# Two edits to a four-layer network: one more product on VectorE in the last pair, and filter rows in four row groups

## The chip, the cores and the metric

The kernel runs on one core of a Trainium2 chip. The core has a matrix engine (TensorE, PE in the profile, with PEld for its weight loads), VectorE (DVE), ScalarE (ACT), GpSimd (POOL) and SyncE (SP), which here only issues transfers. Matmuls write PSUM, a memory taken here in banks of 128 partitions by 512 numbers. The metric is the time on the device in microseconds. Everything is in 32-bit floats.

## What is computed

Eight images of 64 channels and 64 x 64 pixels go through four layers: an attention layer over pixels, two blocks of windowed attention, a layer that filters each pixel with its own 3 x 3 filter (layer 2), and a state-space scan in four directions (layer 3). The change touches layers 2 and 3. Cut to what matters:

```python
# layer 2: nine filter weights for each pixel, times nine for each channel
s = jnp.einsum('bchw,tc->bthw', x, sw) + sb[None, :, None, None]
s = filter_norm(s, axis=1)             # minus the mean of the nine, over their deviation
...
cf = filter_norm(cf, axis=2)           # nine per channel, from the image's mean
for idx in range(TAPS):
    i, j = (idx // K, idx % K)
    out = out + xp[:, :, i:i + H, j:j + W] * s[:, idx:idx + 1] * cf[:, :, idx, None, None]

# layer 3: the scan along each of four directions k, with 16 states n per channel
def step(h, inp):
    u_t, dt_t, B_t, C_t = inp
    h = h * jnp.exp(dt_t[..., None] * A) + dt_t[..., None] * B_t[:, :, None, :] * u_t[..., None]
    return (h, jnp.einsum('bkcn,bkn->bkc', h, C_t))
```

## The kernel before

The images are taken in four pairs. For all of layers 0 to 2 a pair lies in 128 partitions, two images of 64 channels. Layer 3's scans take one image at a time, with its 128 inner channels.

**How the pairs are staggered.** The program first takes pair 0 through layers 0, 1 and 2 and the preparation of its scans, with part of pair 1's layer 0 beside it (`begin`, line 1168). Then, for each pair p, `scans` (line 1644) runs the scans of p, and between its steps it places the work of a second stream: `back` of pair p-1 (what follows the scans in layer 3) and `front` of pair p+1 (layers 0 to 2 and the scans' inputs). Beside the last pair's scans only `back` of pair 2 is left; `back` of the last pair runs alone at the end. The order in which instructions stand on each engine is then fixed by a scheduler when the program is built. It knows which instructions depend on each other and estimates their durations, so an edit can move instructions that it doesn't name.

**Layer 2** (`layer2` of the class `_Direct`, line 1526). It works in eight chunks of 512 pixels, eight rows of the image. In each chunk a matmul makes the centred filter weights, 9 for each of the two images and so 18 rows (`p_m`, line 1540). ScalarE squares them, a second matmul sums the squares (`p_v`, line 1544), four activations turn that into one over the deviation (lines 1547 to 1550), and VectorE makes the filter rows `f` (line 1552). Then there are nine taps. For each, a matmul with a matrix of zeros and constants, `pick`, spreads one row of `f` per image over that image's 64 channels (`pb`, line 1557). VectorE multiplies that with the shifted image and the channel's weight (`tap`, line 1560), and a matmul with the unit matrix adds it up in the bank `acc` (line 1561). After that a 1 x 9 convolution of nine matmuls follows (`py`, line 1571). The banks `p_m`, `p_v` and `pb` share three PSUM buffers, given out by `bank` (line 1199). The tables of the layer are loaded by `load` (line 240) on ScalarE's queue at the layer's start.

**The scans** (`scans` and `step`, line 1714). A unit is one direction k and one stretch of 512 pixels of one image; a unit has eight steps, each for two of the 16 states (j is 0 or 1), so that a pair has 64 units and 512 steps. For a step, SyncE fetches two rows of B and two of C from memory, each broadcast to all partitions (`fetch`, line 1702, 512 KB each; three buffers each), and POOL makes the product `vd` of B with dt times u for both states at once (`products`, line 1709, two steps ahead). For each state ScalarE makes the decay factors `dad` in a PSUM bank (line 1732), VectorE scans (line 1735), and ScalarE keeps the last value for the next unit (`carry`, line 1743). The result is multiplied with C, and TensorE adds it up over the 16 states in the bank `yd` with unit-matrix matmuls (`sums`, line 1762). At the end of a unit VectorE adds `yd` to the image's `Y`.

Who multiplies with C is what the change alters. In the first three pairs, in steps with even number, POOL takes both states in one instruction of 1024 columns (line 1746). In odd steps, and in all steps of the last pair, POOL takes state 0 (line 1748) and VectorE takes state 1 (line 1749). Where VectorE is to multiply, the scan writes over the decay factors in PSUM; where POOL is to, it writes the tile `hd` in SBUF, the memory beside PSUM. The banks of the decay factors come from three buffers, which also serve the two matmuls that prepare a unit (`pdd` and `pbc`).

The two statements in question:

```python
n0, rp = 2 * (i % 8), i % 2 or u["image"] >= B - 2
...
to = da if rp and j else h[:, j]
```

Of the kernel before, what the change touches and what calls it, by code (L numbers as in the profile page):

```python
# [17 lines left out]
P = 128  # L18
CH = 512
# [21 lines left out]
def _dup(a):  # L41
    a = np.asarray(a)
    return np.concatenate([a, a], axis=0)


def _blockdiag(a):
    a = np.asarray(a)
    r, c = a.shape
    out = np.zeros((2 * r, 2 * c), np.float32)
    out[:r, :c] = a  # L50
    out[r:, c:] = a
    return out
# [27 lines left out]

GENERAL = ("xpT", "dtT", "alog", "rpb0", "rpb1", "maskh", "maskv", "norm1_b0", "norm1_b1", "qb0", "qb1", "kb0", "kb1", "vb0", "vb1", "pb0", "pb1", "f1b0", "f1b1", "norm2_b0", "norm2_b1", "smask")
TEMP = ("swbd", "ds")
TABLES = ("cw2T", "pick")
TEMPW = ("xr", "drT", "alogs", "rpbT0", "rpbT1", "maskq", "b_all", "smask_t")


def _pack(w):
# [62 lines left out]
    e9 = np.eye(TAPS, dtype=np.float32)  # L152
    put("swbd", _blockdiag(f["sw"]))
    put("sb", _dup(_col(f["sb"])))
    put("cen9", _blockdiag(e9 - np.float32(1.0 / TAPS)))
    put("var9", _blockdiag(np.full((TAPS, TAPS), 1.0 / (TAPS - 1), np.float32)))
    put("cw1T", _dup(f["cw1"].T))
    mid = f["cw1"].shape[0]
    put("cb1", _col(f["cb1"]))
    put("cw2T", f["cw2"].reshape(C, TAPS, mid).transpose(2, 1, 0))  # L160
    pick = np.zeros((2 * TAPS, TAPS, P), np.float32)
    for im in range(2):
        for t in range(TAPS):
            pick[TAPS * im + t, t, 64 * im : 64 * im + 64] = np.sqrt(2.0) / 3
    put("pick", pick)
    put("cb2", _dup(f["cb2"].reshape(C, TAPS)))
    put("gmask", np.repeat(np.eye(2, dtype=np.float32) / L, 64, axis=0))
    w2 = f["w2"][:, :, 0, :]
# [41 lines left out]
    temp = [x for x in items[n_first:] if x[0] in TEMP]  # L210
    tempw = [x for x in items[n_first:] if x[0] in TEMPW]
    keep = [x for x in items[n_first:] if x[0] not in GENERAL + TEMP + TEMPW + TABLES]
    tables = [(n, sh, a[0 : 2 * TAPS]) for n, sh, a in items if n in TABLES]
    packs, layout = [], []
    for g, part in enumerate((items[:n_first], keep, temp, tempw, late, tables)):
        packs.append(np.ascontiguousarray(np.concatenate([x[2] for x in part], axis=1)))
# [10 lines left out]
class _Net:  # L227
# [45 lines left out]
    def prepare(self):  # L273
        nc, w, const = self.nc, self.w, self.const
        self.eps = const.tile([P, 5], F32, name="eps", tag="eps")
        for i, e in enumerate((LN_EPS, CN_EPS, BN_EPS, 1e-37, 1e-10)):
            nc.gpsimd.memset(self.eps[:, i : i + 1], e)
        eps_bn = self.eps[:, 2:3]

        bn1 = w["bn1"]  # L280
        sc = const.tile([P, 2, C], F32, name="bn1sc", tag="bn1sc")
        self.bn_fold((sc[:, 0, :], sc[:, 1, :]), bn1[:, 0, :], bn1[:, 1, :], bn1[:, 2, :], bn1[:, 3, :], eps_bn)
        self.w1a = const.tile([65, C], F32, name="w1a", tag="w1a")
        nc.vector.tensor_tensor(self.w1a[0:64, :], w["w1T"][0:64], sc[0:64, 0, :], ALU.mult)
        nc.vector.tensor_copy(self.w1a[64:65, :], sc[64:65, 1, :])

        self.w1bd = const.tile([P, P], F32, name="w1bd", tag="w1bd")
        nc.gpsimd.memset(self.w1bd, 0.0)
        for im in range(2):
            lo = slice(64 * im, 64 * im + 64)  # L290
            nc.vector.tensor_tensor(self.w1bd[lo, lo], w["w1T"][lo], sc[lo, 0, :], ALU.mult)
        self.b1row = const.tile([1, 2, C], F32, name="b1row", tag="b1row")
        nc.vector.tensor_copy(self.b1row, sc[0:1, 1, :].unsqueeze(1).to_broadcast([1, 2, C]))
        self.ones = const.tile([P, P], F32, name="ones", tag="ones")
        nc.gpsimd.memset(self.ones, 1.0)
        self.sums = const.tile([P, B // 2, 2, 32], F32, name="sums", tag="sums")

        bn = w["bn23"]
        self.bn23 = const.tile([P, 4], F32, name="bn23", tag="bn23")
        for i in range(2):  # L300
            self.bn_fold(
                (self.bn23[:, 2 * i : 2 * i + 1], self.bn23[:, 2 * i + 1 : 2 * i + 2]),
                *[bn[:, 4 * i + k : 4 * i + k + 1] for k in range(4)],
                eps_bn,
            )

        nr = 2 * TAPS

        self.swc = const.tile([P, nr], F32, name="swc", tag="swc")
        self.sbc = const.tile([nr, 1], F32, name="sbc", tag="sbc")  # L310
        with self.tc.tile_pool(name="psf", bufs=1, space=PSUM) as ps:
            pw = ps.tile([P, nr], F32, name="pswc", tag="pswc")
            nc.tensor.matmul(pw, lhsT=w["swbd"], rhs=w["cen9"], start=True, stop=True)
            nc.scalar.activation(self.swc, pw, AF.Copy)
            pb = ps.tile([nr, 1], F32, name="psbc", tag="psbc")
            nc.tensor.matmul(pb, lhsT=w["cen9"], rhs=w["sb"], start=True, stop=True)
            nc.scalar.activation(self.sbc, pb, AF.Copy)
        self.dsum = const.tile([P, 1], F32, name="dsum", tag="dsum")
        nc.vector.tensor_reduce(self.dsum, w["ds"], AX.X, ALU.add)
# [523 lines left out]
    def layer2(self, X):  # L843
# [5 lines left out]
        with ExitStack() as st:  # L849
# [7 lines left out]
            for c in range(NCH):  # L857
                cols = slice(c * CH, (c + 1) * CH)

                pm = ps.tile([nr, CH], F32, name="ps_m", tag="mm")  # L860
                nc.tensor.matmul(pm, lhsT=self.swc, rhs=X[:, cols], start=True, stop=True)
                q = wk.tile([nr, CH], F32, name="q2", tag="q2")
                nc.scalar.activation(q, pm, AF.Square, bias=self.sbc)
                pv = ps.tile([nr, CH], F32, name="ps_v", tag="pv")
                nc.tensor.matmul(pv, lhsT=w["var9"], rhs=q, start=True, stop=True)

# [3 lines left out]
                nc.scalar.activation(d, d, AF.Ln, bias=self.eps[0:nr, 4:5])  # L870
                nc.scalar.activation(d, d, AF.Exp, scale=-1.0)
                f = wk.tile([nr, CH], F32, name="f2", tag="f2")
                nc.vector.scalar_tensor_tensor(f, pm, self.sbc, d, ALU.add, ALU.mult)

                acc = ps.tile([P, 8, 64], F32, name="acc", tag="acc", bufs=1)
                for t in range(TAPS):
# [272 lines left out]
class _Direct:  # L1149
# [376 lines left out]
    def layer2(self, X):  # L1526
# [6 lines left out]
        with tc.tile_pool(name="w2", bufs=2) as wk:  # L1533
            net.load(wk, (5,))
            cf = net.channel_filters(X, wk, self.pf, "f")
            for c in range(NCH):
                x = X[:, c * CH : (c + 1) * CH]

                pm = self.bank("p_m", (nr, CH))
                nc.tensor.matmul(pm, lhsT=net.swc, rhs=x, start=True, stop=True)  # L1540
                q = wk.tile([nr, CH], F32, name="q2", tag="q2")
                nc.scalar.activation(q, pm, AF.Square, bias=net.sbc)
                pv = self.bank("p_v", (nr, CH))
                nc.tensor.matmul(pv, lhsT=w["var9"], rhs=q, start=True, stop=True)

                d = wk.tile([nr, CH], F32, name="d2", tag="d2")
                nc.scalar.activation(d, pv, AF.Ln, bias=net.eps[0:nr, 3:4])
                nc.scalar.activation(d, d, AF.Exp, scale=0.5)
                nc.scalar.activation(d, d, AF.Ln, bias=net.eps[0:nr, 4:5])
                nc.scalar.activation(d, d, AF.Exp, scale=-1.0)  # L1550
                f = wk.tile([nr, CH], F32, name="f2", tag="f2")
                nc.vector.scalar_tensor_tensor(f, pm, net.sbc, d, ALU.add, ALU.mult)

                acc = self.total("acc", (P, 8, 64))
                for t in range(TAPS):
                    pb = self.bank("pb", (P, 8, 64))
                    nc.tensor.matmul(pb, lhsT=w["pick"][:, t, :], rhs=f, start=True, stop=True)
                    src = XP[:, 8 * c + t // 3 : 8 * c + t // 3 + 8, t % 3 : t % 3 + 64]
                    tap = wk.tile([P, 8, 64], F32, name="tap", tag="tap", bufs=3)
                    nc.vector.scalar_tensor_tensor(tap, src, cf[:, t : t + 1], pb, ALU.mult, ALU.mult)  # L1560
                    nc.tensor.matmul(acc, lhsT=w["ident"], rhs=tap, start=(t == 0), stop=(t == TAPS - 1))
                    yield 2.3
# [151 lines left out]
    def step(self, i, st):  # L1714
# [3 lines left out]
        u = self.units[i // 8]  # L1718
        k, c, at, CC, v = u["k"], u["c"], u["at"], st["C"], st["v"]

        n0, rp = 2 * (i % 8), i % 2 or u["image"] >= B - 2
        rev = k >= 2

        def along(t):
# [4 lines left out]
        for j in range(2):  # L1729
            n = n0 + j  # L1730
            da = self.bank("dad", (P, TD), "da")
            nc.scalar.activation(da, u["du"][:, 0], AF.Exp, scale=net.As[:, k, n : n + 1])  # L1732
            first = 0.0 if at == 0 else self.carries[:, n : n + 1]
            to = da if rp and j else h[:, j]
            nc.vector.tensor_tensor_scan(along(to), along(da), along(v[:, j]), first, ALU.mult, ALU.add)  # L1735
            hs.append(to)
            if at < NTD - 1 and (rp or j):
                ends = h[:, :, 0] if rev else h[:, :, TD - 1]
                cs = self.carries[:, n0 : n0 + 2]
                if rp:  # L1740
                    ends = to[:, 0:1] if rev else to[:, TD - 1 : TD]
                    cs = self.carries[:, n : n + 1]
                nc.scalar.activation(cs, ends, AF.Copy)  # L1743

        if rp == 0:
            st["w"] = nc.gpsimd.tensor_tensor(v, h, CC, ALU.mult)  # L1746
        else:
            st["w"] = nc.gpsimd.tensor_tensor(v[:, 0], h[:, 0], CC[:, 0], ALU.mult)  # L1748
            nc.vector.tensor_tensor(v[:, 1], hs[1], CC[:, 1], ALU.mult)  # L1749

    def sums(self, i, st, after=None):

# [181 lines left out]
```

## Time and profile before

| | |
|---|---|
| median of 3 runs | 13789.17 us (13784.27 to 13789.92) |
| the profiled execution | 13842.86 us, its span 13841.1 us |
| TensorE busy | 11209.6 us, 81% of the span |
| VectorE busy | 8419.5 us, 61% |
| GpSimd busy | 8170.1 us, 59% |
| ScalarE busy | 7076.0 us, 51% |
| pair 0 without scans beside it | from 0 to about 2200 us |
| scans of pairs 0, 1, 2, 3 begin | about 2212, 4728, 8086, 11451 us |
| last pair's scans end, its `back` begins | 13587 us |

The page's 40 slices of 346 us each show how the load moves between engines:

```profile
PE   9999986888887679989888667997898767666665
DVE  0121336777668773366666766337665777987875
POOL 0000005888778755566666775547665688878982
PEclk9999977898898889998888788998888888888887
```

Each digit is the busy share of a slice in tenths, and PEclk is the clock granted to TensorE, in tenths of full speed. Slices 5 and 6 (counted from 1) hold pair 0's layer 2; the stretch from slice 34 on holds the last pair's scans, and the last slice mostly its `back`. A busy share is the union of an engine's instructions in the slice, so it says how long an engine had something running, not how fast that ran. The scans' four stretches can be told by the 512 products with B that POOL makes in each: 512 before 4727.5 us, 512 up to 8085.5, 512 up to 11450.5 and 512 after.

### The profile page before, as it was taken

What the parts mean: (1) busy time and instruction counts of PE and PEld (TensorE: products, weight loads), DVE (VectorE), ACT (ScalarE), POOL (GpSimd) and SP (SyncE); (2) the same over time, 40 slices, a digit from 0 to 9 for tenths busy, and PEclk for the clock granted to TensorE, in tenths of its full rate; (3) what the DMA queues carried; (4) which work ended last, traced back from release to release, by engine and by line L of the source; (5) the groups of instructions that cost most, each with busy time, mean ns of one, the idle gap of its engine ahead of it and who ended that gap; (6) DMA issues with size and microseconds to landing.
All of it is one profiled execution on the core that took longest, in us unless ns stands there. A gap on an engine that the chain in (4) does not pass through costs nothing. (4 is left out here: it accounts for less than half of the span.)

```text
span 13841.1 us, 141364 instructions
## 1 busy us (share of the span) xinstructions
PE 11209.6 (81%) x46358; PEld 4137.2 (30%) x46358; DVE 8419.5 (61%) x9763; ACT 7076.0 (51%) x15475; POOL 8170.1 (59%) x4111
## 2 busy tenths in 40 slices
PE   9999986888887679989888667997898767666665
PEld 2243322334232222224432222223443222222221
DVE  0121336777668773366666766337665777987875
ACT  5556514565536545555544545555554544454442
POOL 0000005888778755566666775547665688878982
PEclk9999977898898889998888788998888888888887
DMA  0000005666667754454554764335544577777882
GB/s 23 1 1 1 1 14 188 232 238 226 215 215 250 247 169 135 140 178 169 173 169 169 241 232 157 131 128 193 183 163 154 198 253 262 270 250 271 278 272 97
DMA packets 705785, 2383.41 MB, mean 172 GB/s; under 512 B 81092, under 2 KB 81220, under 8 KB 704012
## 3 DMA queue, kind: packets, MB, share of 16 engines
q1 hardware_dynamic: 681312, 2319.76, 49.3%
q10 hardware_dynamic: 23724, 54.50, 1.0%
q8 instruction: 367, 6.01, 0.2%
q14 instruction: 382, 3.13, 0.1%
HBM read 2271.18 MB, written 102.76 MB: 172 GB/s over the span
## 5 line engine op out<-in xcount | busy, mean ns | idle before, releaser
L1712 POOL TENSOR_TENSOR vd<-B,du 128x1024 f32<-128x1024 f32 x2048 | 4840.6, 2369 | 3889.7 <-DVE X L1352 2197.2
L1762 PE MATMUL yd<-vd,pack 128*128 128x512 f32 x8192 | 4637.8, 697 | 1386.2 <-POOL vd L1746 574.0
L1735 DVE TENSOR_TENSOR_SCAN hd<-dad,carry,vd 128x512 f32<-128x512 f32 x2464 | 3090.6, 1271 | 1024.6 <-ACT dad L1732 494.7
L1732 ACT ACTIVATE dad<-du,As 128x512 f32<-128x512 f32 x4096 | 2716.2, 680 | 1087.3 <-DVE hd L1735 761.8
L1762 PEld LDWEIGHTS yd<-vd,pack 128*128 128x128 f32 x8192 | 1633.4, 216 | 4072.9 <-issue 1829.8
L1746 POOL TENSOR_TENSOR vd<-hd,C 128x1024 f32<-128x1024 f32 x768 | 1811.9, 2359 | 1212.3 <-DVE hd L1735 618.7
L1748 POOL TENSOR_TENSOR vd<-hd,C 128x512 f32<-128x512 f32 x1280 | 1637.9, 1281 | 297.3 <-DVE hd L1735 217.9
L1302 ACT ACTIVATE e<-s 128x512 f32<-128x512 f32 x2048 | 1201.7, 592 | 1022.4 <-PE s L1296 1020.4
L1735 DVE TENSOR_TENSOR_SCAN dad<-dad,carry,vd 128x512 f32<-128x512 f32 x1120 | 1427.0, 1274 | 119.3 <-POOL vd L1712 79.4
L1296 PE MATMUL s<-X 64*128 64x512 f32 x4096 | 1325.4, 649 | 74.3 <-ACT e L1302 74.1
L1288 PE MATMUL po<-e,VT 128*64 128x512 f32 x4096 | 1197.7, 628 | 13.3 <-ACT e L1302 13.2
L1743 ACT ACTIVATE carry<-hd 128x1 f32<-128x1 f32 (+1 forms) x1792 | 357.7, 202 | 1222.9 <-DVE hd L1735 1218.5
L1749 DVE TENSOR_TENSOR vd<-dad,C 128x512 f32<-128x512 f32 x1280 | 859.7, 672 | 63.9 <-ACT carry L1743 54.0
L1296 PEld LDWEIGHTS s<-X 64*128 64x128 f32 x4096 | 360.1, 187 | 952.6 <-issue 786.1
L1450 PEld LDWEIGHTS w_av<-vals,w_e 64*64 64x64 f32 x16384 | 561.0, 147 | 196.4 <-issue 87.9
L1450 PE MATMUL w_av<-vals,w_e 64*64 64x9 f32 x16384 | 589.3, 208 | 25.5 <-ACT w_e L1440 25.4
L1435 DVE TENSOR_TENSOR w_e<-w_s,bias 128x512 f32<-128x512 f32 x512 | 329.5, 681 | 448.1 <-PE w_s L1423 447.6
L1735 DVE TENSOR_TENSOR_SCAN hd<-dad,vd 128x512 f32<-128x512 f32 x352 | 419.5, 1210 | 174.1 <-ACT dad L1732 78.1
L1440 ACT ACTIVATE w_e<-w_e 128x512 f32<-128x512 f32 x512 | 311.6, 627 | 377.5 <-DVE w_e L1435 265.8
L1743 ACT ACTIVATE carry<-dad 128x1 f32<-128x1 f32 x1120 | 189.1, 169 | 602.5 <-DVE dad L1735 600.3
L1687 PE MATMUL pdd<-xs,xdt 128*128 128x512 f32 x512 | 338.7, 749 | 185.1 <-DVE hd L1735 72.4
L1288 PEld LDWEIGHTS po<-e,VT 128*64 128x64 f32 x4096 | 221.6, 136 | 824.5 <-issue 774.2
(247 smaller groups left out, 10798.1 us busy)
## 6 DMA issues: line engine op xcount, KB each, us to landing
B<-rows SPq DMA_DIRECT2D x2048, 512.0 KB, 5.0
C<-rows SPq DMA_DIRECT2D x2048, 512.0 KB, 4.5
xs<-xt SPq DMA_DIRECT2D x128, 256.0 KB, 3.2
xs<-xc SPq DMA_DIRECT2D x128, 256.0 KB, 3.6
xc<-xcv ACTq DMA_DIRECT2D x64, 256.0 KB, 3.7
zs<-z ACTq DMA_DIRECT2D x64, 256.0 KB, 4.3
xt<-XT ACTq DMA_DIRECT2D x32, 512.0 KB, 7.1
rows<-bc SPq DMA_DIRECT2D x256, 64.0 KB, 2.0
```

The source lines that it names most:

```text
L1288: nc.tensor.matmul(po[half[im]], lhsT=VT[:, t, half[im]], rhs=es[im], start=(t == 0), stop=(t == 31))
L1296: nc.tensor.matmul(ss[im], lhsT=at(half[im], t), rhs=X[half[im], jc * CH : (jc + 1) * CH], start=True, stop=True)
L1302: nc.scalar.activation(e, ss[im], AF.Exp, scale=C**-0.5, accum_out=parts[:, im, t, jc : jc + 1])
L1450: nc.tensor.matmul(self.av[half[im], x % 4 + j, h, :], lhsT=es[h // 4][half[im], j, h % 4, :], rhs=V[half[im], x + j, h, :], start=True, s ...
L1712: self.nc.gpsimd.tensor_tensor(v, st["B"], dx.to_broadcast([P, 2, TD]), ALU.mult)
L1732: nc.scalar.activation(da, u["du"][:, 0], AF.Exp, scale=net.As[:, k, n : n + 1])
L1735: nc.vector.tensor_tensor_scan(along(to), along(da), along(v[:, j]), first, ALU.mult, ALU.add)
L1743: nc.scalar.activation(cs, ends, AF.Copy)
L1746: st["w"] = nc.gpsimd.tensor_tensor(v, h, CC, ALU.mult)
L1748: st["w"] = nc.gpsimd.tensor_tensor(v[:, 0], h[:, 0], CC[:, 0], ALU.mult)
L1749: nc.vector.tensor_tensor(v[:, 1], hs[1], CC[:, 1], ALU.mult)
L1762: m = nc.tensor.matmul(y, lhsT=w["ident"], rhs=st["v"][:, j], start=(n == 0), stop=(n == NST - 1))
```

## The change

It has two parts.

**Layer 2's filter rows in four row groups.** The constant matrix `cen9` is set four times side by side, padded to 32 columns each, so that the centred filter weights come out of one matmul in 128 rows: the same 18 rows, starting at partitions 0, 32, 64 and 96, with rows of zeros between. The activations and the filter rows `f` then work on 128 partitions in place of 18. The variance matrix is its block-diagonal form, `var94`. Tap t takes its rows from group t mod 4, and the table `picks` holds the constants of tap t in that group's rows. The tables that are loaded at the layer's start become 128 rows of 1088 numbers in place of 18 rows of 1728; the matrices that move between the loaded packs (`pick`, `cen9`) change the packs' sizes a little. The class `_Net` has a general path for other inputs, which is not run here; it keeps using 18 rows.

**Who multiplies with C in the last pair.** `rp`, which was true or false, becomes `own`, the number of states of a step that VectorE multiplies. In the first three pairs it is `i % 2`, as before. In the last pair it is 1, and 2 in each fourth step (i mod 4 is 3). In such a step both scans write over the decay factors in PSUM, VectorE makes both products, POOL none, and the tile `hd` is allocated and not written. Of eight products in four steps VectorE thus makes five and POOL three, where it was four and four. `st["w"]`, after which the sums of the step before are put in TensorE's order, is the product for state 0, on whichever engine it is.

```diff
-TEMP = ("swbd", "ds")
-TABLES = ("cw2T", "pick")
+TEMP = ("swbd", "ds", "cen9")
+TABLES = ("cw2T", "picks", "var94")
...
-    put("cen9", _blockdiag(e9 - np.float32(1.0 / TAPS)))
+    cen9 = np.pad(_blockdiag(e9 - np.float32(1.0 / TAPS)), ((0, 0), (0, 32 - 2 * TAPS)))
+    put("cen9", np.tile(cen9, (1, 4)))
...
+        picks[32 * (t % 4) : 32 * (t % 4) + n9, t // 4] = pick[:, t]
+    var9 = items[[x[0] for x in items].index("var9")][2]
+    for g in range(4):
+        four[32 * g : 32 * g + n9, 32 * g : 32 * g + n9] = var9[0:n9]
...
-        self.swc = const.tile([P, nr], F32, name="swc", tag="swc")
-        self.sbc = const.tile([nr, 1], F32, name="sbc", tag="sbc")
+        self.swc = const.tile([P, P], F32, name="swc", tag="swc")
+        self.sbc = const.tile([P, 1], F32, name="sbc", tag="sbc")
...
-                pm = self.bank("p_m", (nr, CH))
+                pm = self.bank("p_m", (P, CH))
                 nc.tensor.matmul(pm, lhsT=net.swc, rhs=x, start=True, stop=True)
-                q = wk.tile([nr, CH], F32, name="q2", tag="q2")
+                q = wk.tile([P, CH], F32, name="q2", tag="q2")
                 nc.scalar.activation(q, pm, AF.Square, bias=net.sbc)
-                pv = self.bank("p_v", (nr, CH))
-                nc.tensor.matmul(pv, lhsT=w["var9"], rhs=q, start=True, stop=True)
+                pv = self.bank("p_v", (P, CH))
+                nc.tensor.matmul(pv, lhsT=w["var94"], rhs=q, start=True, stop=True)
...
                 for t in range(TAPS):
+                    g = slice(32 * (t % 4), 32 * (t % 4) + nr)
                     pb = self.bank("pb", (P, 8, 64))
-                    nc.tensor.matmul(pb, lhsT=w["pick"][:, t, :], rhs=f, start=True, stop=True)
+                    nc.tensor.matmul(pb, lhsT=w["picks"][g, t // 4, :], rhs=f[g], start=True, stop=True)
...
-        n0, rp = 2 * (i % 8), i % 2 or u["image"] >= B - 2
+        n0 = 2 * (i % 8)
+        own = 1 + (i % 4 == 3) if u["image"] >= B - 2 else i % 2
...
-            to = da if rp and j else h[:, j]
+            to = da if j >= 2 - own else h[:, j]
...
-            if at < NTD - 1 and (rp or j):
+            if at < NTD - 1 and (own or j):
...
-        if rp == 0:
+        if own == 0:
             st["w"] = nc.gpsimd.tensor_tensor(v, h, CC, ALU.mult)
-        else:
-            st["w"] = nc.gpsimd.tensor_tensor(v[:, 0], h[:, 0], CC[:, 0], ALU.mult)
-            nc.vector.tensor_tensor(v[:, 1], hs[1], CC[:, 1], ALU.mult)
+        for j in range(2 if own else 0):
+            engine = nc.vector if j >= 2 - own else nc.gpsimd
+            m = engine.tensor_tensor(v[:, j], hs[j], CC[:, j], ALU.mult)
+            if j == 0:
+                st["w"] = m
```

## The prediction

> **What bounds the kernel now.** I read the page for its 40 slices first: no engine is the bound throughout, so each half of the change is judged in its own stage. Then the stage table for layer 2 (four stretches, one for each pair of images) and for the last pair's scans, then the timeline inside one layer-2 chunk, then the groups and waits of the last pair.
>
> Stage table; columns are the stretch, its length, then PE, PEld, DVE, ACT, POOL busy, granted clock, DMA share, GB/s:
>
> ```profile
> 1705.00:2020.00 315.00, 300.18 (x466) 93.92 (x466) 102.91 (x161) 38.47 (x60) 0.00 (x0) 0.72 0.03 13
> 3646.00:4157.00 511.00, 451.61 (x893) 160.33 (x893) 345.17 (x370) 197.17 (x416) 396.33 (x193) 0.92 0.63 212
> 7109.00:7477.00 368.00, 342.69 (x652) 124.12 (x651) 189.31 (x222) 98.29 (x200) 180.31 (x88) 0.87 0.39 134
> 10481.00:10839.00 358.00, 333.67 (x653) 120.94 (x654) 190.06 (x222) 98.28 (x200) 180.70 (x88) 0.90 0.41 138
> 11451.00:13587.00 2136.00, 1420.47 (x2474) 479.53 (x2473) 1777.49 (x1846) 1024.46 (x2350) 1831.92 (x1024) 0.85 0.78 268
> 12400.00:13560.00 1160.00, 751.52 (x1294) 257.80 (x1295) 919.92 (x936) 531.75 (x1268) 1018.89 (x576) 0.85 0.81 275
> 12933.00:12953.00 20.00, 9.61 (x18) 3.26 (x17) 17.03 (x17) 5.95 (x18) 20.00 (x12) 0.91 0.87 296
> 1719.70:1747.70 28.00, 28.00 (x29) 6.99 (x28) 5.23 (x7) 0.00 (x0) 0.00 (x0) 0.50 0.00 0
> ```
>
> In layer 2 TensorE is busy 95%, 88%, 93% and 93% (rows one to four): it is the bound, and time taken off it is time off the path. In the last pair's scans POOL leads (1832 of 2136 us, 86%) with VectorE close (83%). In a steady 20 us POOL has no idle time at all. The last row is a chunk with nothing beside it: TensorE at half clock.
>
> Timeline, first a chunk whose order alternates pick and tap sum, then one that takes them three by three:
>
> ```profile
> 1719.72 2.07 PE L1557 MATMUL pb<-f,pack 18*128 18x512 f32 x2
> 1721.72 2.08 PE L1561 MATMUL acc<-tap,pack 128*128 128x512 f32 x2
> ...
> 1834.94 2.84 PE L1557 MATMUL pb<-f,pack 18*128 18x512 f32 x6
> 1836.10 2.46 DVE L1560 SCALAR_TENSOR_TENSOR tap<-XP,cf,pb 128x512 f32<-128x512 f32 x3 [0.22 <-PE pb L1557]
> 1837.71 4.54 PE L1561 MATMUL acc<-tap,pack 128*128 128x512 f32 x6
> 1842.17 3.10 PE L1557 MATMUL pb<-f,pack 18*128 18x512 f32 x6
> ```
>
> A matmul is two records. Three picks take 2.8 us one after the other, 0.93 each, all on the same 18 rows; the triple's period is 5.5 us at full clock (2.77 + 2.77) and 7.2 here, where half the clock is withheld at times.
>
> The last pair's scans, groups and DVE waits:
>
> ```profile
> L1748 POOL TENSOR_TENSOR vd<-hd,C 128x512 f32<-128x512 f32 x288 | 365.6, 1273 | 83.9 <-issue 49.5 <-DMA C<-rows 21.6 <-DVE hd L1735 11.5
> L1749 DVE TENSOR_TENSOR vd<-dad,C 128x512 f32<-128x512 f32 x288 | 192.3, 668 | 0.1
> DVE hd L1735 <- POOL vd L1712: 120.6, 139, 3.8
> DVE dad L1735 <- POOL vd L1712: 92.4, 76, 3.1
> q1 hardware_dynamic: 92715, 318.35, 80.4%
> ```
>
> The first two are one product with C on either engine; the next two say that VectorE loses 213 us waiting for POOL's products with B; the last is the DMA share over 12400 to 13560.
>
> **What the Trainium skill says.** "TensorEngine Tiling (Array Packing)", Key Properties: tiles of the array on different rows load weights and multiply in parallel; its section on gotchas adds that they must write different PSUM banks. "TensorE: Matmul & The Clock Gate", Part 3, gives 3.07 times for four row tiles of 32. The trace agrees for other row groups: attention's score matmuls with 64 rows, 4096 records of 649 ns, sum to 2658 us and keep TensorE busy for 1325, two at a time. The same page, Part 1: the clock is half or full, by how busy the array has been. The trace shows 0.50 in the alternating chunk although matmuls follow each other without a gap, so few rows seem to count as little work; that is my reading, not a stated fact.
>
> **The change, part by part.** *Layer 2.* The centred matrix, its variance and the filter rows f are now made four times over, at partitions 0, 32, 64 and 96; pick t reads group t mod 4. Width in partitions costs nothing elementwise: Ln on 18 partitions takes 674 ns, on 128 (the norms) 681; Exp 620 against 624; the matmul with 18 rows of weights 662, with 128 rows 671. Wider weight loads (99 to about 206 ns, twice for p_m and p_v) are at worst 32 x 4 x 0.11 = 14 us of weight loading, which runs beside matmuls; I charge 0. The table load grows from 121.5 to 544 KB, four times, on ACT's DMA queue; one was issued at 7080.91 and first read by the matmul at 7092.01, and a 512 KB load of B lands in 5.0 us, so 11 us cover it; uncovered it would cost about 5 each time. Startup's single matmul with 128 columns is under 1 us.
>
> Which picks can overlap is read from the program order of the two kernels. Beside pair 0 the new order has 12 runs of three picks, 4 of two, 28 single; pair 1: 7, 8, 35; pairs 2 and 3: 17, 6, 9 each (unchanged from before except pair 0, by one run). Never more than three, because three banks hold them. So 28 + 22 + 40 + 40 = 130 picks ride beside another.
>
> A triple now: three picks in about one pick's time. The first tap started 1.16 us after the first pick, takes 0.75, so the first sum can start at about 2.0 instead of 2.77; the later taps follow at 0.70, ahead of the sums' 0.93. Saving 0.77 per triple, not 1.86: the tap, hidden before, becomes what is late. At withheld clock more is to be had, up to 7.2 - 4.8 = 2.4, if three row groups at once keep the clock up. Of a pair, other sums follow, so the whole 0.93 goes.
> - Pair 0: 12 triples at 0.77 to 2.4, I take 1.5 = 18; 4 pairs at half clock 1.6 = 6. Together 24.
> - Pair 1: 7 x 0.77 + 8 x 0.93 = 13; TensorE is least bound there and waits 20.6 us for taps behind scans: 8.
> - Pairs 2 and 3: 17 x 1.0 + 6 x 0.93 = 22; times the busy share, and some taps stand behind scans (VectorE 52%): 18 each.
> Sum 68 us. Bounds: +10 (no overlap, loads exposed) to 130 x 0.93 + 12 x 1.66 = -141.
>
> *Last pair.* In every fourth of its 512 steps the first product with C goes from POOL to VectorE: 128 times. POOL loses 128 x 1.27 = 163 us (3.54 to 3.22 a step; 1018.89/288 is 3.54). VectorE gains 128 x 0.62 = 79 us (0.67 less the 0.05 by which neighbours overlap): 3.19 to 3.35 a step. DMA needs 0.804 x 1160/288 = 3.24 a step whatever the engines do. So the floor falls from 3.54 to 3.35, by 0.19, and VectorE and DMA take POOL's place, all within 4%. Steps really take 4.03 (1160/288); nearly 0.5 is lost at each run of eight steps. With three even resources I expect the loss to grow to 0.57: 3.92, saving 0.11 x 290 steps = 32 us after 12400. Before that, back's work makes VectorE busy (up to 288 of 299 us in one stretch) and the 220 steps win about 8: relief of the 213 us of waits against 34 us more work. Sum 40. Bounds: +79 (VectorE's additional work in full) to -110 (0.19 a step, and some of the losses).
>
> Scheduled moves: SP's loads of C wait for VectorE's and POOL's products in turn; in a step with both on VectorE the buffer frees earlier. The h tile is not written in such a step, nothing waits for it. Carries read PSUM instead, 169 against 202 ns on ACT. ACT loads as many tables as before. Beyond the edit, the program order around each run of eight steps changes: before, POOL takes three products with B, one with C, two B, then four C in a row; now three C, then two B. VectorE's updates of Y and du shift by an instruction or two, and some 545 of SP's 7007 transfers stand elsewhere. The shorter burst lets B's products start earlier, the shifted updates could cost as much; I take 0, and 20 us either way is inside the bounds above.
>
> Sum against the profiled execution (span 13841.1, its time 13842.9): -68 - 40 = -108, or 0.78%. The median, 54 us lower, scales to 13682.
>
> **The rivals.** *Layer 2 alone pays.* DMA at 0.95 in its best stretches and VectorE take over from POOL at once. For it: 3.24 and 3.35 stand close. Against: VectorE's 213 us of waits for POOL. -68: 13721.
>
> *The last pair alone pays.* Picks stay serial, or taps behind scans take the gain. Against: the 64-row overlap. -40 and some 10 from pair 0: 13739.
>
> *Slower: banks.* Where both products are on VectorE, both decay factors, overwritten by the scans in PSUM, hold their banks until the products are through, and there are three banks. If the next Exp waits for the second product, VectorE waits for it: 0.62 + 0.68 + 0.1 = 1.4 us, 128 times = 180 us, so +112: 13901. It decides from 0.76 us a step, (68 + 28)/128. For it: ACT waits 73.8 us for line 1749's products already (12400 to 13560). Against: in the new order, the second Exp of the next step needs only the first product; the second product and a scan, 1.8 us, cover its 0.8.
>
> **How the numbers follow.** Forecast 55% (alone 13610 to 13745), layer 2 alone 18%, last pair alone 10%, banks 12%, gains and losses cancelling 5% (13789). A measurement here can tell 0.2%, 28 us, from no change. Faster: 55 + 18 + 6 = 79; slower 12; same 9. Range 13600 to 13790: it leaves out the banks' case and a low tail of 5%.
>
> **What would show it.** Pick triples with records starting within some 10 ns and the first sum at 2.0 us; the four layer-2 stretches shorter by 24, 8, 18, 18 us, pair 0's clock above 0.72. In the last pair POOL near 1670 us busy, VectorE near 1856, waits for line 1712 well under 213, the stretch near 2096. Wrong: serial picks; ACT waiting for line 1749 by over 150 us; VectorE over 95% busy in a stretch that is not shorter.

## The result, and the profile after

| | before | after |
|---|---|---|
| median of 5 runs each | 13789.92 us (13784.27 to 13813.41) | 13702.1 us (13667.8 to 13724.29) |
| the profiled execution | 13842.86 us | 13724.29 us, its span 13722.5 us |

The ratio of the times is 0.9924, with a 95% interval of 0.9904 to 0.9945: the kernel became faster by 0.55 to 0.96%. The forecast was 13682, 20 us below the median.

First the stage table of the kernel after: the four layer-2 stretches, a triple chunk, an alternating chunk, and the last pair's scans. Columns as in the prediction: stretch, length, PE, PEld, DVE, ACT, POOL busy, granted clock, DMA share, GB/s.

```profile
1697.00:1999.00 302.00, 264.75 (x459) 84.86 (x459) 101.63 (x161) 38.99 (x60) 0.00 (x0) 0.73 0.03 13
3606.00:4117.00 511.00, 435.49 (x898) 157.15 (x896) 346.03 (x372) 197.86 (x417) 396.12 (x194) 0.92 0.63 213
7086.60:7428.50 341.90, 291.77 (x658) 108.52 (x658) 188.91 (x224) 98.93 (x201) 180.82 (x88) 0.92 0.43 144
10428.00:10770.00 342.00, 294.07 (x658) 109.09 (x658) 188.86 (x224) 98.80 (x201) 180.83 (x88) 0.92 0.42 144
1859.20:1873.20 14.00, 11.52 (x37) 4.27 (x37) 7.02 (x12) 0.00 (x0) 0.00 (x0) 1.00 0.05 19
1742.00:1770.00 28.00, 27.91 (x28) 6.99 (x28) 5.84 (x9) 0.78 (x1) 0.00 (x0) 0.50 0.00 0
11382.00:13469.00 2087.00, 1418.41 (x2473) 462.79 (x2472) 1849.00 (x1974) 1033.53 (x2350) 1677.47 (x896) 0.86 0.80 274
```

From the first pick to the last convolution, layer 2 takes 299.6, 508.5, 339.8 and 340.0 us in the four pairs, where it took 314.7, 510.3, 368.9 and 358.4: 15, 2, 29 and 18 less, 64 together. TensorE, which was busy 88 to 95% there, is now busy 85 to 88%. The last pair's scans take 2086.9 us, where they took 2135.9: 49 less. 64 and 49 are 113 of the 118.6 us between the two profiled executions. The medians differ by 88: the profiled execution of the kernel before lies 53 us above its median, the one after 22. In the profiles of five more kernels with layer 2 unchanged (experiments 2, 6, 7, 9 and 10) the four stretches together take 1537 to 1556 us, where the kernel before takes 1552; with row groups they take 1488 (the kernel after) and 1475 (experiment 1).

Rows five and six are to be read together. The triple chunk has the full clock though TensorE is idle for a sixth of it, and the alternating one, never idle, has half.

The timeline inside that triple chunk:

```profile
1859.24 1.13 PE L1567 MATMUL pb<-f,pack 18*128 18x512 f32 x6
1860.40 2.06 DVE L1570 SCALAR_TENSOR_TENSOR tap<-XP,cf,pb 128x512 f32<-128x512 f32 x3 [0.22 <-PE pb L1567]
1861.20 2.84 PE L1571 MATMUL acc<-tap,pack 128*128 128x512 f32 x6 [0.83 <-DVE tap L1570]
1863.97 1.14 PE L1567 MATMUL pb<-f,pack 18*128 18x512 f32 x6
```

Three picks, six records, take 1.13 us where they took 2.84; their single records start 7 ns apart. The first sum starts 1.96 us after the first pick. The 0.83 us that TensorE then waits for the tap is the new last wait of a triple. The period is 4.73 us.

The waits in the last pair's scans after (who waited, for whom: us, times, longest):

```profile
DVE dad L1746 <- POOL vd L1722: 74.8, 67, 4.3
DVE hd L1746 <- POOL vd L1722: 50.2, 53, 4.0
POOL vd L1722 <- DMA B<-rows: 127.8, 93, 12.6
ACT dad L1743 <- DVE vd L1760: 203.5, 264, 4.6
DVE hd L1746 <- ACT dad L1743: 14.5, 17, 1.9
DVE dad L1746 <- ACT dad L1743: 10.5, 11, 2.2
```

VectorE's loss to POOL's products with B fell from 213 to 125 us. POOL now waits 128 us for B to land. ScalarE waits 203.5 us for VectorE's products (109.5 before), but VectorE loses only 25 us to ScalarE.

Where in the last pair was the time won? Each group of 32 steps can be dated by the starts of POOL's products with B. The second stream's work ends in step 213 before and in step 225 after; from then on the scans are alone. The first 224 of the 512 steps took 964 us before and 973 after, the next 64 took 259 and 267, so in the first 288 steps 17 us were lost. The next 192 took 771 and 714, so 57 were won; the last 32 took 142 and 133. Why the 64 steps from 224 on, with nothing beside them, won nothing is not known. From here on "late" means the 192 steps from step 288. The late stretch of the kernel before, then of the kernel after:

```profile
12674.20:13445.10 770.90, 502.07 (x866) 175.61 (x864) 612.94 (x622) 352.24 (x838) 681.54 (x385) 0.84 0.81 275
```

```profile
12623.00:13337.00 714.00, 484.81 (x864) 159.63 (x862) 634.58 (x671) 353.47 (x838) 623.11 (x337) 0.88 0.85 297
```

Before, POOL leads with 88% (681.54 of 771), and VectorE has 80%. After, VectorE has 89%, POOL 87%, and the DMA share has risen from 0.81 to 0.85. No single engine leads any more.

### The profile page after: what moved, and what is told of

Same layout as the page of the kernel before. It is cut to its first block, busy times and chain, and to the rows that moved or that the text cites. A ratio compares the mean times of both kernels' runs of the same rounds, so it can differ in the third digit from the quotient of the medians.

```text
span 13722.5 us, 141112 instructions
## 1 busy us (share of the span) xinstructions
PE 11044.8 (80%) x46358; PEld 4075.2 (30%) x46358; DVE 8484.9 (62%) x9891; ACT 7083.5 (52%) x15475; POOL 8012.5 (58%) x3983
## 5 line engine op out<-in xcount | busy, mean ns | idle before, releaser
L1746 DVE TENSOR_TENSOR_SCAN hd<-dad,carry,vd 128x512 f32<-128x512 f32 x2352 | 2948.5, 1271 | 933.8 <-ACT dad L1743 483.4
L1760 POOL TENSOR_TENSOR vd<-hd,C 128x512 f32<-128x512 f32 x1152 | 1473.8, 1280 | 339.7 <-DVE hd L1746 281.1
L1746 DVE TENSOR_TENSOR_SCAN dad<-dad,carry,vd 128x512 f32<-128x512 f32 x1232 | 1562.0, 1274 | 124.4 <-POOL vd L1722 73.2
L1760 DVE TENSOR_TENSOR vd<-dad,C 128x512 f32<-128x512 f32 x1408 | 939.3, 674 | 66.5 <-ACT carry L1754 57.7
```

What stands on the lines that cost most here:

```text
L1760: m = engine.tensor_tensor(v[:, j], hs[j], CC[:, j], ALU.mult)
```

## The experiments

All ratios are against the kernel before, run on the same chip beside each.

**1 and 2: each half alone.** The first kernel is the changed one with the old division in the last pair; the second is the kernel before with the changed `step` alone.

```diff
-        own = 1 + (i % 4 == 3) if u["image"] >= B - 2 else i % 2
+        own = 1 if u["image"] >= B - 2 else i % 2
```

> Layer 2's filter rows in four row groups, the last pair as before. Theory (picks of different row groups overlap, and pair 0's clock stays up where three stand together): 13790 - 65 = about 13725 us; pair 0's layer-2 stretch about 20 us shorter, those of pairs 2 and 3 about 20 to 28 each, that of pair 1 nearly unchanged; the last pair's scans stay at 2136 us. Rival (most of the gain is the last pair's): above 13765.

> Five of eight products with C on VectorE in the last pair, layer 2 as before. Theory: 13790 - 45 = about 13745 us, the last pair's scans near 2090 us, all of it won after back's work has ended (about 116 us for 32 steps in place of 126), nothing or a small loss before. Rival (layer 2 alone pays, VectorE and DMA take POOL's place at once): 13790 within 15.

Layer 2 alone: 13747.94 us (10 runs), ratio 0.9964 (0.9952 to 0.9976), 33 to 66 us. The last pair alone: 13739.81 us (19 runs), ratio 0.9961 (0.9951 to 0.997), 41 to 68 us. The product of the two ratios is 0.9925, the whole change's 0.9924. So the halves add up, as far as these intervals tell, both pay, and both rivals that let one half pay alone fall. In the second kernel the last pair's scans take 2076 us, the first 288 steps 1235 and the late 192 steps 709: as in the whole change, a little is lost early and more is won late.

**3: is it the overlap?** The layer-2 kernel of experiment 1 with 128-row activations and tables kept, but all nine picks in row group 0.

```diff
-        picks[32 * (t % 4) : 32 * (t % 4) + n9, t // 4] = pick[:, t]
+        picks[0:n9, t] = pick[:, t]
...
-                    g = slice(32 * (t % 4), 32 * (t % 4) + nr)
+                    g = slice(0, nr)
...
```

> As the run with layer 2 alone, but all nine picks read row group 0, so that none can ride beside another; rows, tables and activations are as wide. Theory (the overlap is the cause): 13790 within 15, three picks together take 2.8 us as before, pair 0's triples at about 7.2 us. Rival (the fuller array in p_m and p_v keeps the clock up, or the width itself helps): at least half the gain of the run with layer 2 alone, 13757 or less.

13802.01 us (14 runs), ratio 1.0003 (0.9992 to 1.0013). Its timeline in a triple chunk:

```profile
1841.81 2.84 PE L1567 MATMUL pb<-f,pack 18*128 18x512 f32 x6
1844.58 4.54 PE L1571 MATMUL acc<-tap,pack 128*128 128x512 f32 x6
```

Everything of layer 2's edit is there but the overlap, and the gain is gone: three picks take 2.84 us again, and the three sums 4.54, at half clock for a part. The width costs nothing that this run can tell (its interval is -11 to +18 us), and the row groups are the cause.

**4: all picks in triples.** In pair 0 of the changed kernel only every second chunk runs in triples; the others still alternate. This kernel holds TensorE's order to three picks, then three sums, in every chunk (`behind` puts the sum after the third pick).

```diff
+                    m = nc.tensor.matmul(pb, lhsT=w["picks"][g, t // 4, :], rhs=f[g], start=True, stop=True)
...
-                    nc.tensor.matmul(acc, lhsT=w["ident"], rhs=tap, start=(t == 0), stop=(t == TAPS - 1))
+                    taps = taps + [tap] if t % 3 else [tap]
+                    for s in range(3 if t % 3 == 2 else 0):
+                        n = nc.tensor.matmul(
+                            acc, lhsT=w["ident"], rhs=taps[s], start=(t + s == 2), stop=(t + s == TAPS + 1)
+                        )
+                        if s == 0:
+                            net.behind(n, m)
```

> The changed kernel, with each chunk's taps ordered three picks, then three sums, where the changed kernel's order alternates single picks and sums in every second chunk of pair 0. Theory (the alternation of 18 and 128 rows holds the clock at half, and only in these chunks): eight chunks of 28 us in place of four of 28 and four of 45, so pair 0's layer 2 takes about 226 us in place of 292, its clock is over 0.9, and the kernel takes 13702 - 66 = about 13636 us. Rival (the clock is withheld for another reason, such as idle time while picks wait for VectorE): clock near 0.75 there as now, gain under 25 us, 13680 or more.

13618.79 us (5 runs), ratio 0.9876 (0.9858 to 0.9895). The layer-2 stretches are 243.4, 504.6, 324.9 and 327.5 us, 88 less together than in the changed kernel; by the ratios, 0.9924 and 0.9876, the time is about 66 us less, as expected. Pair 0's stretch came out 17 us above what was expected, at a clock of 0.89 where over 0.9 was expected. The stage table and the timeline of this kernel show why:

```profile
1713.00:1956.50 243.50, 194.36 (x471) 73.05 (x470) 93.29 (x145) 34.81 (x52) 0.00 (x0) 0.89 0.04 16
```

```profile
1777.82 1.13 PE L1567 MATMUL pb<-f,pack 18*128 18x512 f32 x6 [3.31 <-DVE f L1561]
1779.78 4.54 PE L1573 MATMUL acc<-tap,pack 128*128 128x512 f32 x6 [0.83 <-DVE tap L1570]
```

At the start of a chunk TensorE waits 3.3 us for the filter rows, and the next three sums take 4.54 us in place of 2.84.

**5: the fifth product late only.** Experiment 4, with VectorE making the second product only from step 288 on, since the steps before it lose.

```diff
-        own = 1 + (i % 4 == 3) if u["image"] >= B - 2 else i % 2
+        own = 1 + (i % 4 == 3 and i >= 288) if u["image"] >= B - 2 else i % 2
```

> The kernel with all triples, but VectorE takes the fifth product only from step 288 of the last pair on, when back's work is done; before that it takes four of eight. Theory (VectorE is the bound while back's work stands beside, so the fifth product costs there about 11 us): the last pair's scans 2070 - 10 = 2060 us, the kernel about 13609 us. Rival (it costs nothing there): 2070 and 13619.

13600.87 us (4 runs), ratio 0.9859 (0.9844 to 0.9874): the interval overlaps that of experiment 4. The last pair's scans take 2062.6 against 2069.6 us, the first 288 steps 1222 against 1227. The direction is the expected one, but the total doesn't settle it.

**6: six of eight.** If VectorE sets the late pace after the change, more work for it must slow that pace. From experiment 2, with two products on VectorE in every second step:

```diff
-        own = 1 + (i % 4 == 3) if u["image"] >= B - 2 else i % 2
+        own = 1 + i % 2 if u["image"] >= B - 2 else i % 2
```

> As the run with the last pair alone, but VectorE takes both products in every odd step, six of eight. Theory (with five of eight VectorE is the bound, 3.35 us a step and 0.28 lost): 3.50 + 0.28, so about 121 us for 32 late steps in place of 116, more before; the last pair's scans about 2125 in place of 2076, the kernel 13785 to 13795. Rival (POOL or the transfers still set the pace at five of eight): 2076 or less, 13740 or less.

13757.59 us (16 runs), ratio 0.9977 (0.9969 to 0.9985); the last pair's scans take 2098 us. The late stretch:

```profile
12656.00:13366.00 710.00, 490.82 (x866) 168.31 (x864) 660.21 (x721) 356.04 (x840) 566.18 (x290) 0.87 0.85 298
```

The same 192 steps of experiment 2:

```profile
12629.80:13339.10 709.30, 492.75 (x865) 165.27 (x863) 635.16 (x672) 353.84 (x839) 623.25 (x337) 0.87 0.85 299
```

VectorE is busy for 660 us where it was busy for 635, POOL for 566 where it was 623, and the steps take 710 where they took 709. More work for VectorE didn't slow this pace, and less for POOL didn't raise it. Both moved in one edit, so a loss and a gain that just cancel are not excluded by this run alone; experiment 7 speaks against that. What is the same in both is the DMA share, 0.85, and near 299 GB/s. In total neither expectation came true: the scans lie between 2076 and 2125. The sixth product's loss lies in the first 288 steps, 1258 against 1235, and 20 of these 23 us in the first 224 (992 against 972), where VectorE also has the second stream's work.

**7: a quarter of the transfers left out.** From experiment 2: in the last pair, odd steps take the C of the step before them, so half the loads of C don't run.

```diff
-            self.fetch(i + 2, steps[i + 2], 1)
+            if p == B // 2 - 1 and i % 2:
+                steps[i + 2]["C"] = steps[i + 1]["C"]
+            else:
+                self.fetch(i + 2, steps[i + 2], 1)
```

> As the run with the last pair alone, but in the last pair each odd step uses the C of the step before it, so that half of C's loads, a quarter of the scans' transfers, are left out. Theory (VectorE sets the late pace, transfers only nearly so): 32 late steps between 113 and 117 us, the last pair's scans 2060 to 2076. Rival (the transfers set it): DMA share under 0.70 and 32 late steps at 110 or less, the scans under 2040.

13603.75 us (4 runs), ratio 0.9867 (0.9852 to 0.9882); the last pair's scans take 1940 us, 136 less than in experiment 2. The late stretch:

```profile
12554.00:13213.00 659.00, 471.60 (x866) 165.21 (x865) 633.80 (x673) 351.93 (x840) 623.19 (x338) 0.89 0.69 243
```

The rival came true. The same work for VectorE and POOL now takes 659 us, not 709, and only here is VectorE the bound, busy 96%. POOL's waits for B fell from 117 us in the last pair to 24, and the 512 KB load of B took 4.4 us from issue to landing (median of the late stretch), where it took 5.9 in experiment 2.

But the edit does two things at once. It takes a quarter of the traffic away, and since a C that is fetched now serves two steps, C's three buffers last for twice as many steps. That the second may count is seen in SyncE's own waits (SPq is its queue). SyncE issues the loads in order and stands still until the buffer of the next one is free. In the late stretch of experiment 2 it waited for the products with C to be made, and so for buffers of C, for 415 us:

```profile
SPq L1707 <- DVE vd L1750: 313.2, 154, 3.3
SPq L1707 <- POOL vd L1750: 102.2, 43, 8.6
```

In the late stretch of this kernel 17 us of such waits are left:

```profile
SPq L1710 <- DVE vd L1753: 16.6, 27, 1.0
```

So this run shows that the loads set the late pace of experiment 2, but not whether it is their rate or the time at which a buffer of C comes free.

**8: filter rows a chunk ahead.** Experiment 5, where the wait of experiment 4 at a chunk's start is filled: the next chunk's centred weights are made before this chunk's last three sums, and its variance and filter rows before this chunk's convolution.

```diff
+                    if t == TAPS - 1 and c + 1 < NCH:
+                        following = centre(c + 1)
...
+                if c + 1 < NCH:
+                    f, m = spread(*following)
...
+                    if t == 0 and c + 1 < NCH:
+                        net.behind(n, m)
```

> As the run with triples and the late fifth product, and each chunk's filter rows are made while the 1 x 9 convolution of the chunk before runs, so that the picks need not wait for four activations. Theory (in a chunk of triples TensorE stands still for 3 to 4 us before its first pick): pair 0's layer 2 shorter by 7 x 4 = 28 us, about 215 in place of 243, pairs 2 and 3 by up to 10 each; the kernel 13565 to 13585 us. Rival (the wait moves to another place, such as banks held by the rows made ahead): 13605 or more.

13523.55 us (5 runs), ratio 0.9806 (0.9793 to 0.9819), about 42 us below what was expected. Its pair 0 in the stage table, and the joint between two chunks in its timeline:

```profile
1708.00:1910.00 202.00, 180.91 (x471) 67.93 (x470) 93.63 (x146) 34.82 (x52) 0.00 (x0) 0.98 0.05 20
```

```profile
1780.69 8.05 PE L1595 MATMUL py<-act,pack 128*128 128x512 f32 x18 [0.56 <-DVE act L1590]
1788.67 1.13 PE L1571 MATMUL pb<-f,pack 18*128 18x512 f32 x6
```

The picks follow the convolution at once, the clock is 0.98, and pair 0's layer 2 takes 201 us, over a third less than before. Against experiment 5 it became 44 us shorter, where 28 were expected, and pair 1's stretch, for which nothing was expected, 19 us (502 to 483).

**9 and 11: is it a lack of buffers?** POOL's waits for B could also come of too few buffers. Experiment 2 with a fourth buffer of B in the last pair, and experiment 8 with the same:

```diff
-        t = st["BC"[s]] = self.sw.tile([P, 2, TD], F32, name="BC"[s], tag="BC"[s], bufs=3)
+        if self.more and s == 0 and i % 4 == 3:
+            t = self.more.tile([P, 2, TD], F32, name="BC"[s], tag="BC"[s])
+        else:
+            t = self.sw.tile([P, 2, TD], F32, name="BC"[s], tag="BC"[s], bufs=3)
+        st["BC"[s]] = t
...
```

> As the run with the last pair alone, with a fourth buffer for B's loads in the last pair (B alone, for want of room); nothing is left out. What the run with half of C's loads left open: are the transfers late because a buffer comes free too late, or because their rate is at its limit? Theory of the buffers: POOL's waits for B's loads fall from 128 us to under 64 and the last pair's scans from 2076 to 2040 or less, the kernel to 13710 or less. Theory of the rate (share 0.85, near what the transfers can do beside each other): scans 2060 or more, kernel 13740 within 15.

> The kernel with rows ahead, with a fourth buffer for B's loads in the last pair. If the buffers are what makes the transfers late, 13524 - 30 = about 13495 us; if the rate is, 13524 within 15.

On experiment 2: 13737.1 us (4 runs), ratio 0.9955 (0.994 to 0.997), not to be told from the 0.9961 of three buffers. The last pair's scans take 2066 us, 10 less, where the theory of the buffers asked for 2040 or less. POOL's wait for B stays, and the late stretch is 6 us shorter:

```profile
POOL vd L1716 <- DMA B<-rows: 116.3, 88, 12.6
```

```profile
12624.90:13328.60 703.70, 488.03 (x866) 162.88 (x865) 635.38 (x672) 353.60 (x840) 622.89 (x337) 0.88 0.87 301
```

On experiment 8: 13517.32 us (5 runs), ratio 0.98 (0.9787 to 0.9814), not to be told from 0.9806; here too the late stretch is 6 us shorter (711 to 705). So a fourth buffer of B brings a little, but not the 50 us of experiment 7. That doesn't show that the rate is the limit. With the fourth buffer of B, SyncE hardly waits for a buffer of B any more (7 us in the late stretch), but 474 us for buffers of C, and B's loads stand behind C's in its queue. A fourth buffer for C was not tried.

**10: the transfers before the change.** The edit of experiment 7 on the kernel before.

> The kernel before, with half of C's loads left out in the last pair (odd steps use the C of the step before). With five of eight products the same cut won 136 us of the last pair's scans. Theory (with four of eight POOL sets the pace at 3.54 us a step, the transfers only in places): clearly less, scans at 2060 to 2100 us against 2136, late groups of 32 steps still at 116 or more. Rival (the transfers set the pace before as well): scans at 2010 or less.

13732.29 us (4 runs), ratio 0.9946 (0.993 to 0.9961); the last pair's scans take 2065 us, 71 less. Its late stretch, then its first 288 steps:

```profile
12588.20:13345.70 757.50, 485.85 (x866) 167.39 (x864) 617.67 (x625) 351.73 (x840) 682.63 (x386) 0.85 0.62 211
11414.20:12588.20 1174.00, 819.29 (x1462) 279.65 (x1462) 1095.43 (x1111) 627.20 (x1391) 1032.69 (x577) 0.86 0.64 213
```

Late, the cut brings 13 us of 771, 12 of them in the first group of 32 steps; from there on a group takes 126 us with or without it (628 and 631 us for five groups). With four products of eight on POOL, the loads didn't set the late pace; POOL, the busiest engine with 88 to 90%, did, as the 57 us won by taking products off it show. In the first 288 steps the cut brings 49 us, all of it in the first 224 (909 against 964): there the loads mattered already.

## Why the prediction was right, point by point

**Layer 2, the mechanism.** For the triples it was right in each detail: picks start 7 ns apart, the first sum comes at 1.96 us (2.0 was predicted), the period is 4.73 (4.77), and the tap is what is late next, with 0.83 us. Experiment 3 shows that the overlap alone brings it. The extra width and the larger tables were costed at nothing, and cost nothing that experiment 3 could tell.

**Layer 2, the size.** 68 us were predicted; alone it brought 33 to 66, so the term was somewhat too large. The four stretches gave 15, 2, 29 and 18 for 24, 8, 18 and 18. In pair 0, with nothing beside it, the parts that failed can be named. Add up the chunks, each from its first pick to that of the next, the last to the end of its convolution. The four triple chunks took 132.8 us before and 118.2 after: 14.6, where 12 triples at 1.5 were to give 18. The four others, of which before one was mixed and three alternated, took 181.9 and now take 181.5, where the four pairs of picks at half clock, 1.6 each, were to give 6. In them the first sums came 2.9 us earlier, since the tap is exposed there too, but there is no mixed chunk any more: all four alternate at half clock. The prediction had seen that the order changes by one run of picks, and put that at nothing. It isn't nothing: the mixed chunk, 42.5 us in this profile, took 31.0 to 42.5 us in the six other kernels that keep the old order (experiment 3 and those with layer 2 unchanged), and an alternating one takes 44.8 to 46.5 now. The clock of the stretch is 0.73, not clearly above 0.72.

For the pairs beside scans a single profile doesn't settle where the rest is. With layer 2 unchanged, six profiles have pair 2 at 358 to 369 us and pair 3 at 357 to 366. Executions of one kernel differ by up to 80 us (13762.99 to 13842.29 among the runs before beside experiment 1), and a stretch of layer 2 that becomes 29 us shorter shortened the scans beside it by 8 in that execution.

**The last pair, the sum.** 40 us were predicted; alone it brought 41 to 68, in the profile 49. The terms on the engines were right: POOL 1677 us busy (1670 was predicted), VectorE 1849 (1856), the waits for POOL's products with B 125, well under 213, the stretch 2087 (2096).

**The last pair, its distribution.** Here two terms failed. 32 us were to come after 12400 us, which is step 220 of the kernel before, and 8 before it. Up to that step the scans took 947 us before and 959 after, from there on 1189 and 1128: 12 lost and 61 won.

The late term held that the loss above the busiest engine's time grows to 0.57 us a step. In the late stretch it shrank, from 0.48 (771/192 = 4.02, against POOL's 3.54) to 0.37 (714/192 = 3.72, against VectorE's 3.35). The early term held that the relief of the waits outweighs 34 us of additional work on VectorE. It didn't. The first 288 steps took 1222 to 1228 us in the six profiles with four of eight there (the kernel before, experiments 1, 3, 5, 8 and 11), 1227 to 1240 in the four with five of eight (the kernel after, experiments 2, 4 and 9), and 1258 with six of eight (experiment 6). So the early loss is about 8 us, not much more than the profiles differ among themselves, and some 33 with twice as many moved products: it grows with VectorE's work. That the sum of 40 came near is in part luck, since the late term was 29 us too small and the early one 20 us too good.

**What takes POOL's place.** The prediction named VectorE (3.35 us a step) and DMA (3.24) together. The runs correct this. Raising VectorE's share to six of eight left the late pace at 710 us (experiment 6), while a quarter fewer loads brought it to 659 (experiment 7), with VectorE 96% busy. So the loads hold a step at 709/192 = 3.69 us, and VectorE comes next at 659/192 = 3.43. What holds the loads stays open: their rate, for which the quicker landing of B in experiment 7 speaks, or the three buffers of C, for which SyncE's 415 us of waits speak. The 3.24 for DMA took the engines' share in the kernel before as if 1.00 could be reached; they reached 0.85. "DMA: Bandwidth & Descriptors" of the Trainium skill, under Specifications, gives a core about 358 GB/s from memory, and the late stretches here stand at 297 to 299, 83% of that. But its section on bandwidth calls this the share of a core whose neighbour streams too, and gives more for a core alone; this kernel runs on one core. In 18 us slices of experiment 2's late stretch the rate lay between 219 and 350 GB/s, so 299 is a mean with gaps in it, and no run shows it to be a ceiling.

**The rival of the banks.** The sign that was to prove the prediction wrong, ScalarE waiting over 150 us for VectorE's products, did appear, with 203.5 us over the whole last pair (109.5 before), and yet the stretch became shorter. The prediction had read its 73.8 us over the part after 12400 alone; there, 12275 to 13443 after, it is 132. Either way the sign was badly chosen: it says that ScalarE is idle, not that anyone waits for it. VectorE's wait for the decay factors, 25 us after and 23 before, is the row that decides.

## What to carry to other kernels

Where a few small matmuls follow each other, put their operands on different row groups, and then make sure that they stand next to each other in the order: the change as it was took 0.8%, and with the chunks in triples and the filter rows a chunk ahead 2.0%. When an engine is relieved, don't take the next busiest engine as the new bound: give that one more work, and the transfers less, and see which moves the pace. Ask of such an experiment what else it changes: leaving out loads also left more buffers free. Judge a wait by who waits for the waiting engine in turn.

## What the hardware showed that was not expected

- TensorE's clock stayed at 0.50 while its matmuls followed each other without a gap (27.91 of 28 us busy), with an 18-row and a 128-row one in turn, and was at 1.00 with three 18-row picks at once and three sums, although TensorE was then idle for 2.5 of 14 us. "TensorE: Matmul & The Clock Gate" of the Trainium skill, Part 1, ties the clock to how busy the array has been; measured here, the time that matmuls run does not decide it alone. Experiment 3 agrees: its triples with all picks in one row group kept TensorE busy for the whole of 14.3 us, at a clock of 0.76. That rows in use at once are counted fits these chunks, but is only argued.
- A wait of 3.3 us before a triple was followed by three sums at 4.54 us (experiment 4); with the wait filled, the stretch's clock went from 0.89 to 0.98 (experiment 8).
- The loads set the pace of experiment 2's late stretch at a mean share of 0.85 of the 16 DMA engines, whether by their rate or by their buffers. With a quarter of them left out, the same 512 KB load of B landed in 4.4 us in place of 5.9. In the kernel before, the same cut brought the late stretch 13 us, as POOL set the pace there.
